# A two-layer Mamba and attention kernel: four pairs of vector calls merged, a convolution history copied by DMA, integer weights converted by ScalarE

## The chip, the cores and the metric

The kernel runs on one core of one Trainium2 chip. The metric is the device time of one execution in microseconds, lower is better. A core has five engines with an instruction queue each: TensorE (PE in the profile, with its weight loads as PEld), VectorE (DVE), ScalarE (ACT), GpSimd (POOL) and SyncE (SP). In this kernel SP issues all DMA transfers. Each engine works through its queue in order and waits for the others by semaphores.

## The reference, cut to what matters

The input `x` has 2 sequences of 2048 tokens with 256 features. Two layers are applied, each as `x = x + s * silu(g)`, where `s` is a sequence mixer and `g` a feed-forward network, both on the normalised `x`.

```python
# layer 0: s = a Mamba block and an MLP, g = an FFN in blockwise FP4 (blocks of 16)
xz = ln(xn) @ in_proj_w;  xi, z = split(xz, 2)              # 512 channels
xc = silu(causal_conv(xi, conv_w, 4 taps) + conv_b)
dt, B, C = split(xc @ x_proj_w, [16, 32])
dt = softplus(dt @ dt_proj_w + dt_proj_b)
h_t = exp(dt_t * A) * h_{t-1} + dt_t * B_t * xc_t           # 512 channels x 16 states, over 2048 steps
y = (sum_n h_t * C_t + D * xc) * silu(z)
s = x' + gelu(ln(x') @ ffn_w1 + b1) @ ffn_w2 + b2           # x' = xn + y @ out_proj_w
g = fp4_linear(silu(fp4_linear(xn, w_gate)) * fp4_linear(xn, w_up), w_down)
x = x + s * silu(g)
# layer 1: s = attention over the first axis (2 positions) with 16 heads, g = three QLoRA blocks
s = attention(xn)
for k in range(3):                                           # weight = (q / 7.5 - 1) * scale, plus a LoRA term
    h = h + qlora(gelu(ln(qlora(h, 2 * k))), 2 * k + 1)
x = x + s * silu(h)
```

The four taps of the convolution reach three tokens back, so each tile of tokens needs the last three columns of `xi` of the tile before: this is the convolution history. The integers `q` of the QLoRA weights come as int32.

## The kernel before

Time is cut into 8 tiles `j` of 256 tokens, for each of the 2 sequences `b`: 16 stages in the order (0,0), (0,1), (1,0) and so on. A stage has these parts:

- `head`: normalisation, input projection, convolution (as matmuls of `xi` with diagonal matrices `cdiag`), `xc`, `dt`, `ux`, and `bc`, the B and C rows, which go to a scratch in DRAM. It runs a stage ahead of the rest. The history of each sequence is kept in the constant tile `hist[b]`; `head` copies it into the first three columns of `xi`, and the last three columns of `xi` back into it.
- `fp4_half`: quantisation of `xn` and the FP4 network. It leaves `sgs`, the `silu(g)` of the two groups of 128 tokens.
- `scan`: 8 scans per stage, 128 in all. For each, SP loads `bcs` (B and C, spread over the partitions), ACT makes `decay` in eight calls, and DVE makes three large calls on `hh`: a product with `ux`, the scan, and a product with C. Then PE transposes the result into `bank_y`, and SP saves the last column into `state` for the next tile. There are two buffers each of `bcs`, `decay` and `hh`.
- `tail`: second normalisation and MLP. Its last lines form layer 0's result `x1` as `sg * s + xt`, with one product and one sum for each group of 128 tokens.
- `second`: layer 1 for 128 tokens of both sequences, twice after each stage with b = 1, so 16 times. The attention part multiplies the queries `pq` of the two sequences by a difference of keys, reduces, takes tanh, multiplies by a difference of values and adds a mean of values.

Ahead of the stages, weights are prepared: FP4 weights are quantised on the chip, and `make_qlora_weights` turns six int32 tiles into float, scales them and folds the LoRA product in.

No engine's order is written out by hand. The class `Recorder` records all calls with their stage; `order` then plans them with a list of costs for each kind of call (`cost`), and issues them in the order of the plan. It starts from priorities by stage (`lead`, `adjust`) and repeats a backward and a forward pass over the recorded calls for each entry of `passes`; the last forward pass gives the order. An entry holds the weights of that pass: among them how much a change of the table on ACT counts against a call (`bonus`), and shifts for single parts of a stage. A change of ACT's function table is planned at `SWITCH = 1.41` us. All recorded calls are issued from one line (579), so the profile tells them apart by the names of their tiles, not by line.

The tiles are allotted by the plan: `sg` has two buffers of 128x256, `xi` has one.

Of the kernel before, what the change touches and what calls it, by code (L numbers as in the profile page):

```python
# [8 lines left out]
F32 = mybir.dt.float32  # L9
I32 = mybir.dt.int32  # L10
BF16 = mybir.dt.bfloat16
AF = mybir.ActivationFunctionType
ALU = mybir.AluOpType
# [4 lines left out]
P = 128  # L18
D = 256
# [3 lines left out]
T = 256  # L23
TG = T // P
FI = 704
FH = FI // 2
BLK = 16
# [555 lines left out]
def tile_two_layers(ctx: ExitStack, tc: tile.TileContext, a: dict):  # L583
    nc = tc.nc
    rec = Recorder(nc, ctx.enter_context(tc.tile_pool(name="shadow", bufs=1, space=DRAM)))
    x = a["x"]
    out = a["out"]
    B, L, _ = x.shape
# [6 lines left out]
    tmp = rec.pool(ctx.enter_context(tc.tile_pool(name="tmp", bufs=1)), 1)  # L595
# [6 lines left out]
    def bank(stream, name):  # L602
        tag = USES.get(stream, stream)
        return ps.tile([P, 512], F32, tag=f"bank_{tag}", name=name, bufs=BANKS[tag], group=stream)
# [24 lines left out]
    def load(name, shape, src):  # L629
        t = const.tile(shape, F32, tag=name, name=name)  # L630
        rec.sync.dma_start(t, src)
        return t
# [77 lines left out]
    hist = [const.tile([P, 4, 3], F32, tag=f"hist{b}", name=f"hist{b}") for b in range(B)]  # L710
# [150 lines left out]
    def make_qlora_weights():  # L861

        scl = load("q_scl", [P, 6, 2, D // BLK], a["scales"].rearrange("i (c p) n -> p i c n", p=P))
        wl = const.tile([P, 6, 2, D], F32, tag="w_l", name="w_l")
        for i in range(6):
            qi = tmp.tile([P, 2, D], I32, tag="t2k_s0", name=f"qi_{i}", bufs=depth["s0"])
            rec.sync.dma_start(qi, a["qweights"][i].rearrange("(c p) d -> p c d", p=P))
            lab = t2k("s0", f"lab_{i}")
            rec.sync.dma_start(lab[0:32, 0:D], a["lora_a"][i])
            rec.sync.dma_start(lab[0:32, D : 2 * D], a["lora_bt"][i])  # L870
            w = t2k("s1", f"wq_{i}").rearrange("p (c d) -> p c d", c=2)
            rec.vector.tensor_copy(w, qi)
            rec.vector.tensor_scalar(w, w, 1.0 / 7.5, -1.0, ALU.mult, ALU.add)
            for c in range(2):
                wv = w[:, c, :].rearrange("p (n k) -> p n k", k=BLK)
                rec.vector.tensor_tensor(
                    wv, wv, scl[:, i, c, :].unsqueeze(2).to_broadcast([P, D // BLK, BLK]), ALU.mult
                )
            for dc in range(2):
                pw = bank("s0", f"pl_{i}_{dc}")  # L880
                rec.tensor.matmul(
                    pw[:, :D], lhsT=lab[0:32, dc * P : (dc + 1) * P], rhs=lab[0:32, D : 2 * D],
                    start=True, stop=False,
                )
                for oc in range(2):
                    rec.tensor.matmul(
                        pw[:, oc * P : (oc + 1) * P], lhsT=w[:, oc, dc * P : (dc + 1) * P],
                        rhs=ident, start=False, stop=(oc == 1),
                    )
                if i % 2:  # L890
                    rec.scalar.copy(wl[:, i, dc, :], pw[:, :D])
                    continue

                mv = statistics("s0", pw[:, :D].unsqueeze(1), 1, f"l_{i}_{dc}")
                rec.vector.tensor_scalar(
                    wl[:, i, dc, :], pw[:, :D], mv[:, 0, 0:1], None, ALU.subtract
                )
        wt["l"] = wl


    def head(b, j, xt):
        nm = f"{b}_{j}"
# [16 lines left out]
        xi = mam.tile([P, 4, T + 3], F32, tag="xi", name=f"xi_{nm}", bufs=1)  # L919
        if j == 0:  # L920
            rec.vector.memset(xi[:, :, 0:3], 0.0)
        else:
            rec.vector.tensor_copy(xi[:, :, 0:3], hist[b])
        for pr in range(2):
            px = bank("m", f"px_{nm}_{pr}").rearrange("p (m t) -> p m t", m=2)
            for mm in range(2):
# [5 lines left out]
                    )  # L932
            rec.scalar.copy(xi[:, 2 * pr : 2 * pr + 2, 3:], px)
        if j < NJ - 1:
            rec.vector.tensor_copy(hist[b], xi[:, :, T : T + 3])
        xc = mam.tile([P, 4, T], F32, tag="xc", name=f"xc_{nm}", bufs=1)
        for pr in range(2):
            pc = bank("m", f"pc_{nm}_{pr}").rearrange("p (m t) -> p m t", m=2)
# [10 lines left out]
        pd = bank("m", f"pxp_{nm}")  # L949
# [107 lines left out]
    def fp4_half(b, j, h):  # L1057

        nm = f"{b}_{j}"
        sgs = []  # L1060
        q = fp4(h["xn"].rearrange("p g d -> p (g d)"), TG * D, f"x{nm}")
        pt = transpose_pair("q", q.rearrange("p (g d) -> p g d", g=TG), f"q{nm}")
        xq = t2k("q", f"xq_{nm}").rearrange("p (c t) -> p c t", c=2)
        rec.scalar.copy(xq, pt)
        for g in range(TG):
            hb = tmp.tile([P, FI], F32, tag="h", name=f"h_{nm}_{g}", bufs=2)
            for hf in range(2):
                w0 = hf * FH
                both = []
                for key in ("w_gate", "w_up"):  # L1070
                    pg = bank("f", f"p{key}_{nm}_{g}_{hf}")
                    for c in range(2):
                        rec.tensor.matmul(
                            pg[:, :FH], lhsT=xq[:, c, g * P : (g + 1) * P],
                            rhs=wt[key][:, c, w0 : w0 + FH], start=(c == 0), stop=(c == 1),
                        )
                    both.append(pg)
                hg = hb[:, w0 : w0 + FH]
                rec.scalar.activation(hg, both[0][:, :FH], AF.Silu)
                rec.vector.tensor_tensor(hg, hg, both[1][:, :FH], ALU.mult)  # L1080
            q = fp4(hb, FI, f"h{nm}_{g}")
            hq = tmp.tile([P, NW, P], F32, tag="hq", name=f"hq_{nm}_{g}")
            for k0, k1 in ((0, 4), (4, NW)):
                pt = bank("f", f"ph_{nm}_{g}_{k0}").rearrange("p (k t) -> p k t", k=4)
                for k in range(k0, k1):
                    rec.tensor.transpose(pt[:, k - k0, :], q[:, CUT[k] : CUT[k] + P], ident)
                rec.scalar.copy(hq[:, k0:k1, :], pt[:, : k1 - k0, :])
            pd = bank("f", f"pdn_{nm}_{g}")
            for k in range(NW):
                rec.tensor.matmul(  # L1090
                    pd[:, :D], lhsT=hq[:, k, :], rhs=wt["w_down"][:, k, :],
                    start=(k == 0), stop=(k == NW - 1),
                )
            sg = tmp.tile([P, D], F32, tag="sg", name=f"sg_{nm}_{g}", bufs=2)
            rec.scalar.activation(sg, pd[:, :D], AF.Silu)
            sgs.append(sg)
        return sgs

    def tail(b, j, h, x2, sgs, x1):
        nm = f"{b}_{j}"  # L1100
# [11 lines left out]
        for fp in range(4):  # L1112
            ph = bank("f", f"ph_{nm}_{fp}").rearrange("p (f t) -> p f t", f=2)
            gl = t2k("f", f"gl_{nm}_{fp}").rearrange("p (f t) -> p f t", f=2)
            for ff in range(2):
                f = 2 * fp + ff
# [5 lines left out]
            for ff in range(2):  # L1122
                f = 2 * fp + ff
# [3 lines left out]
            for ff in range(2):  # L1127
                f = 2 * fp + ff
# [5 lines left out]
        s = t2k("f", f"s_{nm}").rearrange("p (g d) -> p g d", g=TG)  # L1134
        rec.vector.tensor_tensor(s, pf.rearrange("p (g d) -> p g d", g=TG), x2, ALU.add)

        for g in range(TG):
            sg = sgs[g]
            rec.vector.tensor_tensor(sg, sg, s[:, g, :], ALU.mult)
            rec.vector.tensor_tensor(x1[:, g, b, :], sg, h["xt"][:, g, :], ALU.add)  # L1140


    def second(j, g, x1):
        nm = f"{j}_{g}"
# [41 lines left out]
        dkv = t2k(st, f"dkv_{nm}")  # L1186
# [3 lines left out]
        pq = bank(st, f"pq_{nm}")  # L1190
# [3 lines left out]
        vm = bank(st, f"pvm_{nm}")[:, :D]  # L1194
        bias_row(vm, 32, 2 * D, D)
        for c in range(2):
            for bb in range(B):
                rec.tensor.matmul(
                    vm, lhsT=ht[:, c, bb * P : (bb + 1) * P], rhs=wt["qkv"][:, c, 2 * D :],
                    start=False, stop=(c == 1 and bb == B - 1),  # L1200
                )
        ct = t2k(st, f"ct_{nm}")
        e = small.tile([P, 2 * NS], F32, tag="at_e", name=f"e_{nm}", bufs=2)
        for s in range(2):
            rec.vector.tensor_tensor(
                ct[:, s * D : (s + 1) * D], pq[:, s * D : (s + 1) * D], dkv[:, 0:D], ALU.mult
            )
        rec.vector.tensor_reduce(e, ct.rearrange("p (h d) -> p h d", d=BLK), AX.X, ALU.add)
        rec.scalar.activation(e, e, AF.Tanh, scale=0.5 * float(BLK) ** -0.5)
        for s in range(2):  # L1210
            cs = ct[:, s * D : (s + 1) * D]
            rec.vector.tensor_tensor(
                cs.rearrange("p (h d) -> p h d", d=BLK),
                dkv[:, D : 2 * D].rearrange("p (h d) -> p h d", d=BLK),
                e[:, s * NS : (s + 1) * NS].unsqueeze(2).to_broadcast([P, NS, BLK]), ALU.mult,
            )
            rec.vector.tensor_tensor(cs, cs, vm, ALU.add)
        pt = transpose_pair(st, ct.rearrange("p (b d) -> p b d", b=B), f"d{nm}")
        ctt = t2k(st, f"ctt_{nm}").rearrange("p (c t) -> p c t", c=2)
        rec.scalar.copy(ctt, pt)  # L1220
# [83 lines left out]
    h = head(0, 0, x_first)  # L1304
    rec.stage = (0, QUANT)
    make_fp4_weights()
    for i, (j, b) in enumerate(order):
        if b == 0:
            x1 = mam.tile([P, TG, B, D], F32, tag="x1", name=f"x1_{j}")
# [6 lines left out]
        sgs = fp4_half(b, j, h)  # L1316
# [11 lines left out]
        h = following  # L1328
# [32 lines left out]
        (20, 0.5, 0.1, 0.5, 0.12, [(11, 3, 'tensor', 0.138), (3, 0, 'tensor', -0.771), (5, 0, 'scalar', 0.427)]),  # L1361
        (80, 0.1, 0.05, 2, 0.08, []),
        (20, 1, 0.1, 0.5, 0.12, []),
    ]
    rec.issue(tc, lead=(12.22, -6.26, 0, -7.42, 1.15), bonus=193.318, ahead=0.034, adjust=adjust, passes=passes)

# [47 lines left out]
```

## Time and profile before

| | us |
|---|---|
| median of 3 runs | 1744.28 (1741.94 to 1745.17) |
| the profiled execution: its own time | 1740.26 |
| its span (first to last instruction) | 1738.5 |
| DVE busy | 1629.0 (94%) |
| PE busy | 1554.3 (89%) |
| ACT busy | 1472.7 (85%), of it 467.0 table loads (364) |
| first scan, last scan (start) | 56.8, 1609.2 |

Busy is the time in which an engine had at least one instruction in work. In a row for a group of instructions, the name left of the arrow is the tile written and those to the right are read; after the first bar stand the busy time of the group in us and the mean of one instruction in ns, after the second the idle time of the engine just ahead of them and what ended it. A row of the windows gives, for a stretch, the busy time of each engine, with the number of instructions in brackets, then TensorE's granted clock, the share of the DMA engines and GB/s.

### The profile page before, as it was taken

The page shows a single profiled execution, that of the slowest core. Times are in us where ns is not written, and L with a number is a line of the kernel's source. Part 1 is how long each engine was busy: PE and PEld are TensorE (multiplying, and loading weights), DVE is VectorE, ACT ScalarE, POOL GpSimd, SP SyncE. Part 2 cuts the span into 40 slices and gives each one's busy share as a digit, 9 for nine tenths or more (in the row PEclk, how much of TensorE's full clock was granted, in tenths as well). Part 3 has the DMA queues.
Part 4 walks back from the last instruction along what each step waited for, and adds up shares of the span by engine and source line. Part 5 has one row for each costly group of instructions (what it writes and reads, how often), then busy time and mean ns, then how long its engine had stood idle before and what let it go on. Part 6 is the DMA issues. An engine that isn't in the chain of part 4 may idle for free.

```text
span 1738.5 us, 22023 instructions
## 1 busy us (share of the span) xinstructions
PE 1554.3 (89%) x7948; PEld 1224.5 (70%) x7948; DVE 1629.0 (94%) x1658; ACT 1472.7 (85%) x2903; POOL 180.2 (10%) x122
## 2 busy tenths in 40 slices
PE   7546978899899999989998999999899989997996
PEld 5335757687686868678785777787676767776765
DVE  8999999999999999999999999999999999999623
ACT  6546877779899999989998989999999998999443
POOL 0000100111110111100101002110202011200000
PEclk9768989999999999999999999999999999999999
DMA  7322121212212222222222221222122121111000
GB/s 182 94 57 49 39 55 44 49 40 55 42 50 62 37 52 48 56 43 50 50 50 62 48 45 46 54 43 56 38 49 50 44 56 43 50 43 50 6 6 13
DMA packets 179467, 87.23 MB, mean 50 GB/s; under 512 B 131575, under 2 KB 145565, under 8 KB 179358
## 3 DMA queue, kind: packets, MB, share of 16 engines
q1 hardware_dynamic: 179358, 85.83, 21.3%
q8 instruction: 62, 1.02, 0.2%
q14 instruction: 47, 0.39, 0.1%
HBM read 80.62 MB, written 4.72 MB: 49 GB/s over the span
## 4 chain that ended last, share of the span: by engine, by line
PE 28%; DVE 19%; ACT 11%; issue 6%; POOL 0%; ACTq 0%; DVEq 0%
DVE hh L579 13%; PE bank_f L579 11%; PE bank_m L579 6%; PE bank_s L579 5%; PE bank_y L579 4%; ACT L579 4%; ACT decay L579 3%; ACT t2k_s L579 2%; PE bank_h L579 2%; DVE fp_l L579 2%; DVE fp_sc L579 1%; DVE t2k_s L579 1%; ACT t2k_f L579 1%; DVE h L579 1%; ACT dt L579 0%
## 5 line engine op out<-in xcount | busy, mean ns | idle before, releaser
L579 DVE TENSOR_TENSOR_SCAN hh<-decay,hh 128x2056 f32<-128x2056 f32 x128 | 567.3, 4432 | 4.0 <-ACT decay L579 1.9
L579 ACT ACT_TABLE_LOAD x364 | 467.0, 1283 | 22.0 <-DVE hh L579 8.2
L579 ACT ACTIVATE decay<-dt,amat 128x256 f32<-128x256 f32 x1024 | 443.4, 501 | 48.8 <-DVE hh L579 47.2
L579 PE MATMUL bank_y<-ident,hh 128*128 128x128 f32 x2048 | 280.3, 283 | 48.1 <-DVE hh L579 43.4
L579 PEld LDWEIGHTS bank_y<-ident,hh 128*128 128x128 f32 x2048 | 246.1, 146 | 86.8 <-issue 43.8
L579 DVE TENSOR_TENSOR hh<-ux,bcs 128x2048 f32<-128x2048 f32 x128 | 291.7, 2279 | 2.9 <-PE bank_y L579 2.7
L579 DVE TENSOR_TENSOR hh<-hh,bcs 128x2048 f32<-128x2048 f32 x128 | 292.0, 2282 | 0.4
L579 POOL TENSOR_TENSOR ln_sq_s<-ln_sq_s,power 128x2 f32<-128x2 f32 x42 | 73.1, 1741 | 713.6 <-ACT ln_sq_s L579 713.6
L579 PE MATMUL bank_f<-w_f,t2k_f 128*128 128x256 f32 x512 | 129.6, 384 | 6.8 <-ACT t2k_f L579 6.7
L579 PE MATMUL bank_f<-t2k_f,w_f 128*128 128x256 f32 x512 | 122.9, 381 | 1.4 <-ACT t2k_f L579 1.1
L579 PE MATMUL bank_m<-xi,cdiag 128*128 128x256 f32 x512 | 123.5, 379 | 0.7 <-ACT xi L579 0.7
L579 PEld LDWEIGHTS bank_f<-w_f,t2k_f 128*128 128x128 f32 x512 | 93.2, 191 | 25.5 <-ACT t2k_f L579 11.7
L579 PEld LDWEIGHTS bank_f<-t2k_f,w_f 128*128 128x128 f32 x512 | 95.3, 190 | 18.1 <-ACT t2k_f L579 3.7
L579 PEld LDWEIGHTS bank_m<-xi,cdiag 128*128 128x128 f32 x512 | 94.4, 190 | 15.5 <-ACT xi L579 1.1
L579 PE MATMUL bank_f<-w_down,hq 128*128 128x256 f32 x384 | 97.7, 393 | 4.7 <-ACT hq L579 4.6
L579 PE MATMUL bank_h<-t2k_s,w_l 128*128 128x256 f32 x360 | 88.6, 385 | 9.9 <-ACT t2k_s L579 9.9
L579 DVE SCALAR_TENSOR_TENSOR fp_l<-fp_h,fp_l 128x704 f32<-128x704 f32 (+2 forms) x124 | 91.5, 738 | 5.2 <-ACT fp_h L579 4.6
L579 PE MATMUL bank_f<-w_gate,t2k_f 128*128 128x352 f32 x256 | 91.7, 479 | 4.9 <-ACT t2k_f L579 3.1
L579 PE MATMUL bank_f<-w_up,t2k_f 128*128 128x352 f32 x256 | 90.0, 468 | 6.7 <-DVE h L579 3.7
L579 PEld LDWEIGHTS bank_f<-w_down,hq 128*128 128x128 f32 x384 | 73.3, 197 | 22.5 <-ACT hq L579 8.7
L579 PE MATMUL bank_s<-w_qkv,t2k_s 128*128 128x256 f32 (+1 forms) x280 | 83.8, 432 | 4.0 <-DVE t2k_s L579 4.0
L579 PE MATMUL bank_s<-w_l,t2k_s 128*128 128x256 f32 x336 | 82.6, 384 | 4.5 <-ACT t2k_s L579 4.5
(191 smaller groups left out, 2454.5 us busy)
## 6 DMA issues: line engine op xcount, KB each, us to landing
bcs<-bc SPq DMA_DIRECT2D x128, 512.0 KB, 4.8
xt<-in_x_dram SPq DMA_DIRECT2D x16, 256.0 KB, 3.8
out_dram<-t2k_s SPq DMA_DIRECT2D x15, 256.0 KB, 2.2
w_f<-in_ffn_w_dram SPq DMA_DIRECT2D x2, 1024.0 KB, 9.7
state<-hh SPq DMA_DIRECT2D x112, 4.0 KB, 2.3
t2k_s<-in_qweights_dram SPq DMA_DIRECT2D x6, 256.0 KB, 5.9
w_in<-in_in_proj_w_dram SPq DMA_DIRECT2D x1, 1024.0 KB, 5.4
h<-in_w_gate_dram SPq DMA_DIRECT2D x6, 128.0 KB, 2.2
```

What stands on the lines that cost most here:

```text
L579: getattr(getattr(self.nc, engine), method)(*args, **kwargs)
```

## The change

1. `tail`: product and sum of layer 0's end are made for both groups in one call each. `sgs` is one tile of 128x2x256 with one buffer instead of two of 128x256.
2. `second`: the product of queries and keys and the sum with `vm` are made for both sequences in one call each; the operand that both share is spread by a stride of zero. The product with `e` stays in two calls.
3. `head`: the copies of the history into and out of `xi` become DMA transfers on SP (14 each way; the first tile of a sequence still has a memset).
4. `make_qlora_weights`: the conversion of the integers moves from DVE to ACT (6 calls).
5. `passes` gets five more entries, so the plan is another one for all engines.

```diff
@@ make_qlora_weights
-            rec.vector.tensor_copy(w, qi)
+            rec.scalar.copy(w, qi)
@@ head
-            rec.vector.tensor_copy(xi[:, :, 0:3], hist[b])
+            rec.sync.dma_start(xi[:, :, 0:3], hist[b])
...
-            rec.vector.tensor_copy(hist[b], xi[:, :, T : T + 3])
+            rec.sync.dma_start(hist[b], xi[:, :, T : T + 3])
@@ fp4_half
-        sgs = []
+        sgs = tmp.tile([P, TG, D], F32, tag="sg", name=f"sg_{nm}", bufs=1)
...
-            sg = tmp.tile([P, D], F32, tag="sg", name=f"sg_{nm}_{g}", bufs=2)
-            rec.scalar.activation(sg, pd[:, :D], AF.Silu)
-            sgs.append(sg)
+            rec.scalar.activation(sgs[:, g, :], pd[:, :D], AF.Silu)
@@ tail
-        for g in range(TG):
-            sg = sgs[g]
-            rec.vector.tensor_tensor(sg, sg, s[:, g, :], ALU.mult)
-            rec.vector.tensor_tensor(x1[:, g, b, :], sg, h["xt"][:, g, :], ALU.add)
+        rec.vector.tensor_tensor(sgs, sgs, s, ALU.mult)
+        rec.vector.tensor_tensor(x1[:, :, b, :], sgs, h["xt"], ALU.add)
@@ second
-        for s in range(2):
-            rec.vector.tensor_tensor(
-                ct[:, s * D : (s + 1) * D], pq[:, s * D : (s + 1) * D], dkv[:, 0:D], ALU.mult
-            )
+        rec.vector.tensor_tensor(
+            ct.rearrange("p (s d) -> p s d", s=2), pq.rearrange("p (s d) -> p s d", s=2),
+            dkv[:, 0:D].unsqueeze(1).to_broadcast([P, 2, D]), ALU.mult,
+        )
...
-            rec.vector.tensor_tensor(cs, cs, vm, ALU.add)
+        rec.vector.tensor_tensor(
+            ct.rearrange("p (s d) -> p s d", s=2), ct.rearrange("p (s d) -> p s d", s=2),
+            vm.unsqueeze(1).to_broadcast([P, 2, D]), ALU.add,
+        )
@@ passes
         (20, 1, 0.1, 0.5, 0.12, []),
+        (30, 0.02, 0.02, 1, 0.05, []),
+        (80, 1, 0.05, 1, 0.12, []),
+        (110, 0.1, 0.0, 1, 0.12, []),
+        (30, 1, 0.0, 1, 0.05, [(11, 3, 0.08)]),
+        (30, 0.3, 0.0, 0.3, 0.08, [(0, 3, 'scalar', 0.793), (0, 4, 'gpsimd', 0.705), (12, 4, 'tensor', -0.188), (14, 4, 'tensor', 1.073), (9, 4, 'vector', -0.14)]),
```

More of the change, by code (lines that the diff above doesn't have):

```diff
@@ L1210, in second @@
         for s in range(2):
-            cs = ct[:, s * D : (s + 1) * D]
             rec.vector.tensor_tensor(
-                cs.rearrange("p (h d) -> p h d", d=BLK),
+                ct[:, s * D : (s + 1) * D].rearrange("p (h d) -> p h d", d=BLK),
                 dkv[:, D : 2 * D].rearrange("p (h d) -> p h d", d=BLK),
```

## The prediction

> **What bounds the kernel now.** I read four views in this order: the page's busy shares, the table of windows (busy time by stretch), the waits of the Vector engine, and the chain of waits at the end.
>
> ```profile
> PE 1554.3 (89%) x7948; PEld 1224.5 (70%) x7948; DVE 1629.0 (94%) x1658; ACT 1472.7 (85%) x2903; POOL 180.2 (10%) x122
> ```
>
> DVE leads, but three engines are close, and an average hides the stages. The windows (busy us, then the number of instructions in brackets) cut the span into start, three parts of the main stretch, and end:
>
> ```profile
> 0.00:57.00 57.00, 45.89 (x216) 33.88 (x216) 47.64 (x163) 38.09 (x77) 4.12 (x15) 1.00 0.70 181
> 57.00:450.00 393.00, 306.66 (x1496) 237.38 (x1497) 389.44 (x338) 288.44 (x565) 30.44 (x25) 0.88 0.21 49
> 450.00:1200.00 750.00, 712.65 (x3739) 569.18 (x3737) 738.54 (x683) 703.50 (x1383) 82.15 (x44) 0.99 0.23 49
> 1200.00:1605.00 405.00, 374.56 (x1984) 296.54 (x1983) 393.92 (x353) 385.74 (x770) 54.60 (x26) 1.00 0.20 49
> 1605.00:1739.00 134.00, 114.56 (x516) 87.52 (x516) 59.51 (x125) 56.90 (x112) 8.90 (x12) 0.93 0.03 8
> ```
>
> Columns three to six are PE, PEld, DVE and ACT. From 57 us (first scan) to 1605 us DVE works 1521.9 of 1548 us, 98%: there a microsecond taken from DVE is a microsecond of time, unless another engine takes its place. The next is ACT: 73% busy up to 450 us, but 94% and 95% after it. The waits of DVE inside 57 to 1605 us are short and mostly on PE; none names a DMA:
>
> ```profile
> DVE t2k_s L579 <- PE bank_s L579: 4.6, 4, 2.4
> DVE hh L579 <- PE bank_y L579: 2.7, 3, 1.6
> DVE hh L579 <- ACT decay L579: 1.9, 2, 1.2
> ```
>
> The last 134 us are another regime: DVE 44% busy, PE 85%. In the chain PE runs without a break for most of 1605 to 1670 us, and then two instances of `second` run out as a chain of short steps over all engines:
>
> ```profile
> 1655.30 1.74 PE bank_f L579 x8
> 1657.06 0.48 ACT t2k_f L579
> 1657.59 12.35 PE bank_f L579 x56
> ```
>
> [...] The trace has the 1283, but between an ACT instruction and the load after it the chain shows 0.02 us, so I price a load at 1.28. [...]
>
> **The change part by part.** Counts are those of the two built programs' instruction lists; prices are these rows (busy and mean ns stand after the bar):
>
> ```profile
> L579 DVE TENSOR_TENSOR sg<-sg,t2k_f 128x256 f32<-128x256 f32 x32 | 12.8, 418 | 0.1
> L579 DVE TENSOR_TENSOR x<-sg,xt 128x256 f32<-128x256 f32 x32 | 12.8, 416 | 0.1
> L579 DVE TENSOR_TENSOR sz<-bank_y,sz 128x512 f32<-128x512 f32 x32 | 21.8, 683 | 0.4 <-PE bank_y L579 0.2
> L579 DVE CAST t2k_s<-t2k_s 128x512 f32<-128x512 int32 x6 | 2.5, 418 | 0.0
> L579 DVE COPY xi<-hist 128x12 f32<-128x12 f32 x14 | 2.3, 164 | 0.0
> L579 DVE COPY hist<-xi 128x12 f32<-128x12 f32 x14 | 2.2, 155 | 0.4 <-ACT xi L579 0.4
> L579 ACT ACT_TABLE_LOAD x364 | 467.0, 1283 | 22.0 <-DVE hh L579 8.2 <-PE bank_f L579 3.8 <-PE bank_h L579 1.7
> L579 ACT ACTIVATE fp_h<-fp_l 128x512 f32<-128x512 f32 x16 | 10.0, 627 | 0.1
> ```
>
> 1. DVE, 98 instructions fewer. Durations overlap: in the timeline the next instruction starts about 0.08 us before the end of the one before, so from start to start a 256-wide one takes 0.34, a 512-wide one 0.60, a 12-wide copy 0.10 and a conversion 0.38 us. Four merges of 32 into 16 calls: 64 x (0.68 - 0.60) = 5. Conversions: 6 x 0.38 = 2.3. History: 28 x 0.10 = 2.8. Together 10; by the rows' means it would be up to 17, the upper bound. A broadcast operand already stands in the two large `hh` products at the plain rate, so I add nothing for it.
> 2. ACT, 6 copies of 128x512 more at up to 0.63: under 4 us. Nobody wrote the other addition: the planner issues everything in a new order, and in it ACT loads its table 398 times instead of 364. 34 x 1.28 = 44; together +47.
> 3. SP, 28 DMAs more, 14 reading and 14 writing `hist`. SP is in order. It mostly waits for `hh` products, and an issue takes it about 0.4 us, so the issues themselves (11 us) cost nothing. The landing, by the nearest row, is 2.3 us instead of the copy's 0.16. The write has a whole stage of time. The read has to be in `xi` before the convolution matmuls, next to the two ACT copies into the same tile, but it waits until the head before has finished with `xi`.
>
> ```profile
> bcs<-bc SPq DMA_DIRECT2D x128, 512.0 KB, 4.8
> state<-hh SPq DMA_DIRECT2D x112, 4.0 KB, 2.3
> ```
>
>    Behind a waiting read stand the next `state` and `bcs` transfers, and for `bcs` waits the product that opens a scan. In the timeline the shortest time from the end of a product with `bcs` to the start of the one that needs the refilled buffer is 5.7 us, often 6.6 to 7; issue and landing take 5.2. The cover is thin where scans follow each other closely. In the new order, nearly all reads stand one scan or more after the matmuls they wait for, so I take 0, with bounds of 0 and 14 x 1.5 = 21. A gain is excluded, as no transfer is taken away.
> 4. POOL keeps its 127 instructions, PE its 5610.
> 5. Where the new order puts the work, summed from start-to-start durations. Ahead of the first scan DVE has 39 us instead of 45. The first scan also needs `bcs`, which landed at 53 us just ahead of the 54.2 us start; of its 12 earlier queue entries since `bc` 7 remain, so it should come sooner, but I count 2 us of the 6 as lost. After the last scan starts, DVE has the same (51). PE, from the transposes of the third scan from the end, has 119 us instead of 111: the second `second` of j=6 begins later. About 4 us of it fit into gaps in which PE waited after 1600 us. So +4.
> 6. Stalls of DVE. In stretches of 8 scans ACT's own work was at most 103.3 us where DVE had 93.9; now the worst is 103.8 against 97.9. Counting how far ACT's and PE's work runs ahead of DVE's, scan by scan, beyond a slack of 8 us, the sum falls from 37 to 27 (ACT) and from 57 to 41 (PE): ACT has more work, laid more evenly. The planner also charges 1.41 us for a table load that takes 1.28, so ACT should be early rather than late by its plan. I take -2 of today's 26 us of stalls; bounds -10 and +20.
>
> Sum: -10 (DVE) +2 (start) +4 (end) -2 (stalls) = -6 us. The profiled execution took 1740.26 us (span 1738.5 and 1.8 around it), which gives 1734. The median of the three runs, 1744.28, is 4.0 above it; the same difference on that gives **1738**. Where cover is gone: with 35 of the 47 us after 450 us, ACT has some 25 us of idle time left of 65, and the next late thing would be `decay`.
>
> **The rivals.**
> A. ScalarE becomes the bound (slower). After 450 us ACT idles 65 of 1155 us, most of that waiting for PE results that no reordering removes. If only half of the added 35 us finds room, the other 17 stretch the main part: -6 + 17 = +11, 1755 us. For it: in 1200 to 1605 us, where ACT is at 95%, DVE falls from 98.5% to 97.3%. Against it: the scan-by-scan count above, and DVE's waits on `decay` are only 1.9 us. It decides from 6 us of lost room.
> B. The new history reads hold SP's queue and `bcs` comes late. Against it: DVE never waits for `bcs` today. If a third of the 14 reads cost 1.5 us each: +7, 1745 us.
> C. The end eats it: the extra 8 us on PE count in full, and the later start of `second` adds another 2 of chain: -10 + 2 + 10 - 2 = 0, 1744 us. For it: PE is saturated there.
> D. The plan keeps DVE fuller than I think (10 us of stalls gone): -14, 1730 us.
>
> **How the numbers follow.** Forecast 0.40, D 0.17, A 0.22, B 0.09, C 0.12. About 0.2%, 3.5 us, is what a measurement of this kernel can tell from no change. Faster by more: the forecast and D, but for the forecast's edge near 1741: 0.55. Same: that edge, C and part of B: 0.17. Slower: A and the rest of B: 0.28. The range takes in D with the larger DVE saving and A: 1726 to 1756; the likeliest side alone is 1726 to 1741.
>
> **What would show it.** DVE busy about 1617 us with 1560 instructions; ACT busy about 1519 with 398 loads; the last scan 8 to 12 us earlier; the time from it to the end some 4 us longer. I am wrong if DVE's waits on ACT (`decay`, `fp_h`, `at_e`) grow past 15 us (A), if DVE waits for DMA `bcs` (B), or if the last scan is 8 us earlier and the end is not (C).

## The result, and the profile after

The kernel after takes **1755.86 us** (median of 4 runs, 1755.06 to 1756.99) where the kernel before took 1744.72 in the same set: ratio 1.0066, 95% interval 1.0048 to 1.0083. It is slower by 0.66%, about 11 us. Its profiled execution took 1755.89 us, span 1754.0, so span stands against span as 1738.5 to 1754.0, +15.5. This is 4 us more than the difference of the medians, because the profiled execution of before lay 4 us under its median.

The busy shares first, the same line of the page as shown for before:

```profile
PE 1560.1 (89%) x7944; PEld 1234.8 (70%) x7948; DVE 1613.0 (92%) x1560; ACT 1520.7 (87%) x2943; POOL 175.7 (10%) x122
```

DVE has 16 us less to do and ACT 48 us more, where the prediction had 10 and 47. Then the windows (PE, PEld, DVE, ACT in columns three to six):

```profile
57.00:450.00 393.00, 312.97 (x1538) 242.93 (x1537) 390.31 (x338) 310.48 (x583) 22.25 (x24) 0.88 0.23 51
450.00:1200.00 750.00, 707.54 (x3712) 569.34 (x3714) 728.93 (x639) 724.02 (x1408) 84.96 (x46) 0.98 0.23 49
1200.00:1605.00 405.00, 373.48 (x1952) 296.20 (x1951) 386.26 (x329) 380.54 (x745) 55.32 (x25) 0.98 0.20 47
1605.00:1754.00 149.00, 126.98 (x585) 96.79 (x585) 66.44 (x119) 71.77 (x142) 9.02 (x13) 0.95 0.03 11
```

From 450 to 1605 us DVE fell from 98.1% busy to 96.6%. Work went away, and idle time took its place. The waits of DVE from 57 to 1605 us say for whom it idles:

```profile
DVE hh L579 <- PE bank_y L579: 16.0, 13, 4.7
DVE h L579 <- PE bank_f L579: 6.6, 5, 3.2
```

Each row gives the sum in us, the number of waits and the longest. The first was 2.7 us in 3 waits before, the second 2.2 us in 3; waits on `decay` are gone, and no wait on `bcs` has come. The rows of the merged calls and of the table loads:

```profile
L579 DVE TENSOR_TENSOR sg<-sg,t2k_f 128x512 f32<-128x512 f32 x16 | 10.9, 684 | 0.1
L579 ACT ACT_TABLE_LOAD x398 | 510.6, 1283 | 17.6 <-PE bank_h L579 3.4 <-PE bank_f L579 2.6 <-DVE hh L579 2.4
```

The merged calls cost what the row of a 512-wide call said: 684 ns against 683, and 676 and 675 where one operand is spread by a stride of zero. In the chain of waits there is something that the chain of before does not have: GpSimd's `ln_sq_s`.

```profile
1569.29 2.23 ACT decay L579 x6
1573.06 6.48 POOL ln_sq_s L579
...
1598.58 4.02 POOL ln_sq_s L579
```

`ln_sq_s` is the root of layer 1's normalisation, a call on 128x2 numbers.

The ledger of the traces, in us. It adds up: the last scan starts when VectorE's work and idle time before it are over. VectorE's work counts overlapping instructions once.

| | DVE work before the last scan | DVE idle before the first scan | DVE idle from the first to the last scan | last scan starts | from there to the end |
|---|---|---|---|---|---|
| before | 1573.7 | 9.4 | 26.2 | 1609.2 | 129.2 |
| after | 1557.8 | 16.0 | 45.9 | 1619.7 | 134.3 |

So 16 us of work went, 26 us of idle time came, 6.6 of it before the first scan, and the end is 5 us longer.

### The profile page after: what moved, and what is told of

It is laid out like the page before. It is cut to its first block, busy times and chain, and to the rows that moved or that the text cites. A ratio compares the mean times of both kernels' runs of the same rounds, so it can differ in the third digit from the quotient of the medians.

```text
span 1754.0 us, 22010 instructions
## 1 busy us (share of the span) xinstructions
PE 1560.1 (89%) x7944; PEld 1234.8 (70%) x7948; DVE 1613.0 (92%) x1560; ACT 1520.7 (87%) x2943; POOL 175.7 (10%) x122
## 4 chain that ended last, share of the span: by engine, by line
PE 45%; DVE 29%; ACT 16%; issue 8%; POOL 1%; DMA 1%; ACTq 0%; DVEq 0%
DVE hh L579 19%; PE bank_f L579 17%; PE bank_m L579 11%; PE bank_s L579 8%; PE bank_y L579 6%; ACT L579 6%; ACT decay L579 4%; DVE fp_l L579 3%; PE bank_h L579 2%; ACT t2k_s L579 2%; DVE fp_sc L579 1%; DVE t2k_s L579 1%; ACT t2k_f L579 1%; POOL ln_sq_s L579 1%; DVE h L579 1%
## 5 line engine op out<-in xcount | busy, mean ns | idle before, releaser
L579 PE MATMUL bank_y<-ident,hh 128*128 128x128 f32 x2048 | 287.0, 284 | 46.6 <-DVE hh L579 46.5
L579 POOL TENSOR_TENSOR ln_sq_s<-ln_sq_s,power 128x2 f32<-128x2 f32 x42 | 83.3, 1984 | 738.1 <-ACT ln_sq_s L579 738.1
L579 PE MATMUL bank_h<-t2k_s,w_l 128*128 128x256 f32 x360 | 97.7, 415 | 19.8 <-ACT t2k_s L579 19.6
L579 PEld LDWEIGHTS bank_h<-t2k_s,w_l 128*128 128x128 f32 x360 | 69.2, 205 | 40.6 <-ACT t2k_s L579 29.1
L579 PE MATMUL bank_f<-w_down,hq 128*128 128x256 f32 x384 | 92.9, 383 | 1.4 <-ACT hq L579 1.2
```

What stands on the lines that cost most here:

```text
L579: getattr(getattr(self.nc, engine), method)(*args, **kwargs)
```

## The experiments

The change mixes edits and a new order, so the two were separated by replaying. `order` was made to write down its result (the sequence of calls, and the buffer of each tile); other kernels then follow that list instead of planning:

```diff
-        order, _ = self.order(**how)
+        order = self.follow(plan, slots)    # recorded from the kernel before, or after
```

A merged call stands where the first of its two stood, a call whose operands aren't there yet goes as soon as they are. The added lines move the one issuing line to L671, L695, L726 or so. Single executions vary (the kernel before ran from 1737 to 1754 us over all sets), so each ratio is to the runs of before on the same chip.

| label | calls | order | us | ratio, 95% interval |
|---|---|---|---|---|
| f_all | all edits | before | 1747.14 | 1.0030 (1.0019 to 1.0041) |
| f_merge | merges only | before | 1741.46 | 0.9995 (0.9987 to 1.0003) |
| f_hist | history by DMA only | before | 1747.16 | 1.0027 (1.0017 to 1.0036) |
| f_histw | history writes by DMA only | before | 1747.19 | 1.0021 (1.0010 to 1.0032) |
| f_hist1 | f_hist, writes of j=0 on DVE | before | 1744.35 | 1.0012 (0.9998 to 1.0025) |
| f_conv | conversion on ACT only | before | 1748.09 | 1.0016 (1.0003 to 1.0030) |
| f_loads | none, 36 more table loads | before | 1792.04 | 1.0286 (1.0268 to 1.0304) |
| b_less | none, 34 fewer table loads | before | 1742.51 | 0.9996 (0.9987 to 1.0005) |
| b_pe | none, two taps fewer | before | 1746.13 | 0.9992 (0.9978 to 1.0005) |
| g_none | no edit | after | 1751.85 | 1.0051 (1.0039 to 1.0063) |
| g_less | none, 34 fewer table loads | after | 1753.22 | 1.0058 (1.0042 to 1.0074) |
| g_pe | none, two taps fewer | after | 1761.21 | 1.0093 (1.0066 to 1.0120) |
| g_recip | none, six roots on DVE | after | 1753.79 | 1.0065 (1.0048 to 1.0082) |
| a_recip | all edits, six roots on DVE | after | 1747.21 | 1.0022 (1.0012 to 1.0032) |
| a_nohist | all but the history | after | 1757.43 | 1.0077 (1.0052 to 1.0103) |
| x_oldpass | all edits | planned by the 18 old passes | 1768.33 | 1.0152 (1.0130 to 1.0174) |

### Edits or order

> All four edits, but every engine's queue in the order of the kernel before (no planning: the old order is replayed, merged calls stand where the first of the two stood). Theory 1 (the new order is the loss, through ScalarE's 34 extra table loads and later deliveries to TensorE): faster than before by the DVE work taken away, 10 to 16 us, about 1732; table loads 364. Theory 2 (the edits themselves cost, history reads on SP or the conversion on ACT at the start): slower than before, up to +11, about 1750 to 1756. If it is within 3 us of before, the DVE work taken away turned into waits even in the old order.

> None of the four edits, but every engine's queue in the order of the kernel after (replayed; split calls stand next to each other). Theory 1 (order): slower than after by the DVE work that comes back, 1756 + 5 to 16 = 1761 to 1772, with 398 table loads. Theory 2 (edits): back at before's 1745. If DVE's extra stalls in the new order are slack made by other engines, its work fills them and the time stays near 1756.

Both cost. The new order with the old calls is 0.51% slower (9 us), and the edits in the old order are 0.30% slower (5 us). Theory 1 was right that the order loses and wrong that the edits gain. In f_all VectorE has 5.2 us less to do before the last scan, but idles 12 us more (47.8 instead of 35.6), 6.5 of it before the first scan.

### The merges

> The merged calls of tail and second alone, in the order of before. By start-to-start durations 64 x (0.68 - 0.60) = 5 us less, by row means 9: 1735 to 1740 where DVE paces; no change if merging only moves the wait for the second half (the merged product starts when both halves are there).

Neither end of it: 0.05% faster, not told apart from no change. In the trace, the time from each of these calls to the start of the next one was summed over the four main groups: 42.6 us before (120 calls) and 39.9 with them merged (60 calls); waits in front of the next call are in both sums. So 2.6 us, half of the 5 in the prediction. In three of the groups a merged call held DVE for 0.62 to 0.66 us on average until the next one started, not for 0.60; in the trace of after, the next call starts 0.72 or 0.73 us after a merged product when it reads all of its result (seven times), and mostly 0.58 to 0.61 us after it when it does not. Before, the other half of the product could stand between. It is also the fastest version tried that computes everything; none beats the kernel before by more than the measurement can tell.

### The history

```diff
-            rec.vector.tensor_copy(hist[b], xi[:, :, T : T + 3])
+            rec.sync.dma_start(hist[b], xi[:, :, T : T + 3])     # f_hist, f_histw; f_hist1: only for j > 0
```

> The history by DMA alone, in the order of before. Free (prediction's step 3): -3 to -4.5 us, about 1741. Rival B (reads hold SP's queue, bcs late): +7 or more, about 1752, with waits of DVE for DMA bcs in the trace.

> Order of before; the history is written by DMA (14 on SP), read by VectorE as before. If the write is what costs (it waits in SP's in-order queue behind weight loads and holds the only xi buffer until it has landed, so ScalarE's next copy into xi waits): nearly all of f_hist's loss, first scan 3 to 5 us later than before's 56.8, time about 1746 to 1747. If the reads cost (rival B as predicted): first scan unchanged, time about 1742 to 1743.

> Order of before; history by DMA both ways, but the two writes of j=0, which fall in the start when SP issues weight loads without a break, stay on VectorE. If the loss is the start's queue: first scan within 1 us of 56.8 and time 1741 to 1744 (what is left is f_hist's other 1.6 us of later waits less VectorE's 26 copies). If every write costs alike: 12/14 of the loss stays, about 1746.

The write costs; for the reads no price shows: f_histw has nearly all of f_hist's loss (the difference is inside the intervals), and no wait of DVE names `bcs`. The timeline of f_hist has the place, first SP's queue, then ACT's (start, duration, and in brackets the wait in front):

```profile
37.42 0.73 SPq L671 DMA_DIRECT2D l_bet<-in_ln_beta_dram  x1
38.25 0.77 SPq L671 DMA_DIRECT2D hist<-xi  x1
```

```profile
40.55 0.59 ACT L671 COPY xi<-bank_m 128x512 f32<-128x512 f32 x1 [3.56 <-DMA hist<-xi]
```

`xi` of the first tile was complete at 19.7 us, but the write stands in SP's queue behind the weight loads that SP issues one after the other in the start. In before, SP's transfers follow each other there from 29.5 to 50.9 us without a gap of more than 0.12 us, and one load alone held the queue for 5.47 us. `xi` has one buffer, so the next `head` may fill it only when the write has landed: ACT waits 3.56 us, the convolution and the table loads behind it move, and the first scan starts at 61.5 instead of 56.8 us. With the two writes of j=0 back on DVE (f_hist1) the first scan is at 56.7 and nothing waits for a DMA of `hist`; the rest, +0.12%, isn't told apart from nothing. By time alone f_hist1 isn't told apart from f_hist either (the intervals meet); it is the traces that place the loss in the start.

> The kernel after in its own order, with the history back on VectorE (28 small copies, no DMA). If the history's DMAs cost in the new order as in the old one: 3 to 5 us faster than after, about 1751. If they are free there (first scan of after and g_none are within 0.1 us): VectorE's 28 copies come back, +0 to +3, unless they shift the two GpSimd roots at the end out of VectorE's scan, which would give up to -8.

In the new order the history's DMAs show no price: taking them out of the kernel after gains nothing (1.0077 against 1.0066, the intervals overlap and could hide some 0.2%), and nothing in the trace of after waits for `hist`. The same edit costs 0.27% in one order and nothing that shows in another.

### The conversion

> The integer conversion on ScalarE alone, in the order of before. By the sum of the other edits (f_all 4.2 less f_hist 4.2 plus f_merge -1.4): +1 to +2, about 1745; prediction's step 1 and 2: -2 from VectorE, nothing from ScalarE, 1741 to 1742. A later first scan with a wait of VectorE for ACT t2k_s would show the cost.

About +2.8 us, with an interval that nearly reaches nothing. In the trace VectorE waits 2.5 us for ACT `t2k_s` in the start, and the first scan starts at 60.9 us instead of 56.8; TensorE's granted clock up to 57 us was 0.97 there instead of 1.00, so whether that wait is the whole price isn't shown. In the new order no price shows: VectorE waits 3.12 us for `t2k_s` in the start of after, but the first scan starts at 57.2, and at 57.3 in g_none, which converts on DVE.

### ScalarE's table loads

```diff
+                if i in extra:      # f_loads: 20 places, 36 loads
+                    self.nc.scalar.activation(dum, eps, extra[i])
+                if i in less:       # b_less, g_less: 17 short runs of another table
+                    args[2] = AF.Identity
```

> Calls and order of before, with 20 tiny activations (128x1, into a tile nobody reads) of another function put into ScalarE's queue, spread as the extra work of the new order is: 36 more table loads, 400 in all, 46 us of loads and about 4 us of activations. If ScalarE's load is what makes the new order slow: about as slow as the new order with the old calls, +7 to +12, 1750 to 1755. If ScalarE has room for it (prediction's step 6): within 3 us of before, 1743 to 1746; then the order's loss has another cause.

> Old calls in the order of before, 17 short runs made Identity in the same way: 330 loads instead of 364, 44 us less. Says whether ScalarE's loads are on the path of before too: f_loads lost 48 us for 50 added. VectorE idles only 26 us between first and last scan, so the gain is bounded by about 26: if ScalarE paces together with VectorE, 1720 to 1735; if it has been hidden behind VectorE all along, 1741 to 1745.

> Old calls in the order of after (as g_none, 1751.85), but 17 short runs of silu, gelu or tanh-gelu between calls of another table become Identity (values change, the calls and their sizes stay): 364 table loads, as before, instead of 398, 44 us less. If the 34 loads are the price of the new order (rival A): at or below before's time, 1735 to 1745. If the order loses elsewhere (end +4, start, TensorE): no more than 3 us of it comes back, 1748 to 1752.

Adding 50 us to ACT in the old order costs 48, far outside both numbers expected, so at these places ACT had no room for work that the plan doesn't know of. But taking 44 us away gains nothing in either order. The busy shares of g_none and then g_less show that the work really went:

```profile
PE 1558.0 (89%) x7948; PEld 1230.4 (70%) x7948; DVE 1622.3 (93%) x1658; ACT 1517.3 (87%) x2937; POOL 173.7 (10%) x122
```

```profile
PE 1560.9 (89%) x7948; PEld 1234.5 (71%) x7948; DVE 1622.3 (93%) x1658; ACT 1473.8 (84%) x2903; POOL 174.5 (10%) x122
```

This speaks against rival A, the slower side of the prediction: with as many loads as before, the new order is as slow as with 34 more. It isn't the last word. The 17 places are spread over the kernel and are not those at which the new order added its loads, and between scan 119 and the last none was taken (19 loads in g_none and in g_less, 22 in before). That the plan had put its loads where ACT could bear them fits the three runs, but is argued.

### TensorE

In the trace of g_none, DVE idles 16.0 us more than in before up to the last scan (51.6 instead of 35.6), and its waits on PE between the first and the last scan grow from about 12 to 23 us. A typical one, PE's queue in the timeline:

```profile
593.40 1.25 PE L671 MATMUL bank_y<-ident,hh 128*128 128x128 f32 x10
594.49 0.63 PE L671 MATMUL bank_f<-w_f,t2k_f 128*128 128x256 f32 x2
...
600.79 1.03 PE L671 MATMUL bank_f<-w_f,t2k_f 128*128 128x256 f32 x4
601.65 0.60 PE L671 MATMUL bank_f<-ident,fp_l 128*128 128x128 f32 x4
602.09 1.15 PE L671 MATMUL bank_y<-ident,hh 128*128 128x128 f32 x9
```

and DVE's:

```profile
602.95 2.29 DVE L671 TENSOR_TENSOR hh<-ux,bcs 128x2048 f32<-128x2048 f32 x1 [2.67 <-PE bank_y L671]
```

PE doesn't wait here; 7.6 us of other work, mostly matmuls of the MLP and of layer 1, stand between the first transposes into `bank_y` and the next ones, and DVE needs that buffer for the next scan. Is it PE's amount of work?

```diff
-                for k in range(4):
+                for k in (0, 3):        # b_pe, g_pe: two of the four taps
```

> Order and calls of before, two of the convolution's four taps left out (128 matmuls of 0.44 us, 56 us of TensorE, spread over the 16 heads; values change). If TensorE is not what VectorE waits for in this order: within 3 us of before, 1740 to 1744.

> Old calls in the order of after (g_none, about 1752 to 1753), the same taps left out. If the new order's loss is TensorE's work standing ahead of what VectorE waits for (its waits on PE grow from 9 to 21 us between first and last scan): falls by 6 us or more further than b_pe does, to 1740 to 1746. If the loss is the end and the start alone: as little as b_pe, 1749 to 1753.

This was **inconclusive**. PE's busy time fell by only 34 and 27 us instead of 56 (256 of the 512 records of `bank_m<-xi,cdiag` are left out, and in before 32 of them take 7.08 us), while the granted clock from 450 to 1200 us went from 0.99 to 0.98 in b_pe and 0.97 in g_pe, and g_pe came out slower than g_none. A lighter PE gained nothing that can be told, but a slower clock was part of the experiment. In b_pe it shows in the start too: up to 57 us the granted clock was 0.82 instead of 1.00, and the first scan started at 63.5 us instead of 56.8.

The clock itself is a rival that no run separates. The five executions of g_none were granted 0.956 of the clock on average, the 46 of before in the same set 0.959; but among the 43 of before in another set the fastest (1738.22 us) had 0.966 and the slowest (1753.83 us) 0.956, with one and the same order. Whether a lower clock makes an execution longer or comes with it is not shown.

### GpSimd

```diff
-                rec.gpsimd.tensor_tensor(y, y, power[:, :B], ALU.pow)
+                rec.vector.reciprocal(y, y)     # for j = 6 only, six calls
```

> The kernel after in its own order, but the six inverse roots ln_sq_s of layer 1 for j=6 are made by VectorE as plain reciprocals (1/v in place of v to the -0.5, so layer 1's values for j=6 change) instead of by GpSimd. In the trace of after two of them took GpSimd 6.47 and 4.01 us because VectorE was in a scan, and ScalarE waited 4.5 and 2.5 us for them. If that is what loses VectorE's lead at the end: ScalarE's waits for POOL ln_sq_s after 1570 us go, the last scan starts 6 to 8 us earlier, time 1748 to 1750. If the chain has other work as late: no more than 2 us, 1754 to 1756.

> Control for a_recip: old calls in the order of after (g_none, 1751.85), the six roots of j=6 as reciprocals on VectorE. In the trace of g_none these six take GpSimd 1.0 to 1.7 us and nobody waits for them. If a_recip's gain of 8 us is the two long ones of after: no change here, 1750 to 1754. If GpSimd roots cost in general: 1744 to 1747.

In these two kernels the six calls of j=6 give the reciprocal instead of its root. This is the clearest result. On the edited calls it gains 0.44% (1.0066 to 1.0022, 7.7 us), on the old calls in the same order nothing that can be told (1.0051 and 1.0065, the intervals overlap). The roots of g_none, and then those of after, in the timeline:

```profile
1579.41 1.62 POOL L671 TENSOR_TENSOR ln_sq_s<-ln_sq_s,power 128x2 f32<-128x2 f32 x1 [8.47 <-ACT ln_sq_s L671]
1598.61 1.29 POOL L671 TENSOR_TENSOR ln_sq_s<-ln_sq_s,power 128x2 f32<-128x2 f32 x1 [17.57 <-ACT ln_sq_s L671]
```

```profile
1573.06 6.47 POOL L579 TENSOR_TENSOR ln_sq_s<-ln_sq_s,power 128x2 f32<-128x2 f32 x1 [10.82 <-ACT ln_sq_s L579]
1598.58 4.01 POOL L579 TENSOR_TENSOR ln_sq_s<-ln_sq_s,power 128x2 f32<-128x2 f32 x1 [19.05 <-ACT ln_sq_s L579]
```

And what followed in after, on ACT, PE and DVE:

```profile
1579.57 0.84 ACT L579 ACTIVATE t2k_s<-bank_s,ln_sq_s 128x256 f32<-128x256 f32 x2 [4.50 <-POOL ln_sq_s L579]
```

```profile
1580.46 0.66 PE L579 MATMUL bank_s<-ident,t2k_s 128*128 128x128 f32 x4 [2.73 <-ACT t2k_s L579]
...
1591.31 1.91 PE L579 MATMUL bank_y<-ident,hh 128*128 128x128 f32 x16
```

```profile
1593.26 2.29 DVE L579 TENSOR_TENSOR hh<-ux,bcs 128x2048 f32<-128x2048 f32 x1 [4.68 <-PE bank_y L579]
```

The root runs long, ACT and everything behind it in its queue waits, PE gets `t2k_s` and `t2k_f` late, the transposes of `hh` come late, and DVE stands still for 4.68 us. One more step lies between: TensorE idled 2.73 and 1.51 us here, and from 1582 to 1588 us its granted clock was 0.50, where g_none and a_recip have 1.00. The same six matmuls in after and then in g_none:

```profile
1582.73 2.93 PE L579 MATMUL bank_f<-w_f,t2k_f 128*128 128x256 f32 x6 [1.51 <-ACT t2k_f L579]
1584.50 1.53 PE L671 MATMUL bank_f<-w_f,t2k_f 128*128 128x256 f32 x6
```

Counted from 0, scan 123 of after starts 6.4 us ahead of that of g_none (1574.6 against 1581.0); this was the gain of the edits. Scan 127, the last, starts 1.9 us behind (1619.7 against 1617.8). a_nohist shows the same two roots at 6.46 and 3.87 us, g_less and g_pe the short ones, so it isn't a chance of one execution.

g_recip leaves the roots of earlier tiles alone, and one of them is in the way in both kernels. In g_none:

```profile
1432.49 5.89 POOL L671 TENSOR_TENSOR ln_sq_s<-ln_sq_s,power 128x2 f32<-128x2 f32 x1 [15.12 <-ACT ln_sq_s L671]
```

ACT waits 3.61 us for it, then DVE 2.34 us for PE `bank_f`, and from scan 112 to scan 120 DVE idles 7.9 us where before has 3.1. Over the whole span ACT's waits for `ln_sq_s` are 1.1 us in before, 5.0 in g_none, 12.0 in after and 3.6 in a_recip. So a part of the 9 us of the order may be of this kind; no run took that root out.

### The added passes

> All four edits, planned by the 18 old passes alone, so a third order (405 table loads by its list). If the five added passes are what makes after slow: 1738 to 1748. If it is the edits, or more than 364 loads in any order: 1752 or more.

The edits planned by the 18 old passes alone give 1768.33 us. So the five passes help, against planning the edited calls without them. The edited calls run fastest in the order of before (f_all, 1.0030).

## Why the prediction was wrong, by its own steps

It forecast 6 us less, and the kernel takes 11 us more. The sixth term, VectorE's stalls, failed most; the start in the fifth failed too.

1. **DVE, -10.** 15.9 us went before the last scan, for two reasons. With the order alone DVE's work fell by 7.5 (1573.7 to 1566.2). That is mostly more overlap of neighbours: over the whole span its busy time fell by 6.7, the sum of all its durations by 2.3 only (1739.6 to 1737.3). The edits took 8.4 in the new order (1566.2 to 1557.8) and 5.2 in the old one. The size of the edits was about right, the term of the merges was half of what it was put at, and the overlap that came with the order was not in the term.
2. **ACT, +47.** 48.0 measured, 398 loads. DVE's waits on ACT did not grow past 15 us for the three tiles that it named, and taking as many loads out again (g_less) gave nothing back.
3. **History, 0.** No price of the reads shows, as worked out. "The write has a whole stage of time" was wrong: its buffer has no stage of time, since `xi` is single, and in f_hist ACT waits 3.56 us for it. That SP mostly waits, so that the issues cost nothing, isn't so in the start, where its transfers follow each other up to 50.9 us in before. In this new order no price of the miss shows; in the old one it is +0.2%.
4. **POOL and PE, counts unchanged.** True, and yet a miss. A count says nothing of GpSimd's duration: two calls of the same count and shape took 7.6 us longer (6.47 and 4.01 instead of 1.62 and 1.29).
5. **Start +2, end +4.** The end is 5.1 us longer; that was right, and g_none alone has 4.1 of it (133.3 instead of 129.2). The start was not. The +2 meant that the first scan would come 4 us earlier, as DVE had 6 us less to do ahead of it. DVE did have 6.2 us less (41.2 instead of 47.4), but idled 6.6 us more, and the first scan came 0.4 us later: the term measures +6.6. `bcs` was not sent sooner either: it was issued at 48.30 us instead of 48.08, because `bc` ahead of it went out at 43.00 instead of 39.81. The chain of waits to the first scan of after runs for 8.44 us through PE `bank_m`, and in the first part of it TensorE was at about half its clock. The windows of before, then of after:

```profile
38.00:48.00 10.00, 10.00 (x54) 8.45 (x53) 5.49 (x19) 8.08 (x21) 0.00 (x0) 1.00 0.33 77
38.00:48.00 10.00, 4.76 (x12) 3.55 (x13) 4.72 (x17) 8.08 (x21) 0.00 (x0) 0.55 0.12 16
```

   g_none has 0.51 there, so it comes with the order. What it costs no run shows.
6. **Stalls, -2, with bounds -10 and +20.** This is the step that failed most. Between the first and the last scan DVE idled 45.9 us instead of 26.2: +19.7, at the upper bound. 11.1 of it come with the order (g_none, 37.3), and 8.6 more with the edits in it. From scan 120 to the last, DVE idled 0.9 us in before, 1.2 in g_none and 9.3 in after, and 1.3 in a_recip: this part is shown to come from GpSimd's roots of j=6. I had counted how far ACT's and PE's work ran ahead of DVE's in stretches of 8 scans. That can't see what stands in front of one transpose inside a stretch, and it left GpSimd out.

Put side by side, the four terms DVE, start, end and stalls were -10, +2, +4, -2 and measure -15.9, +6.6, +5.1, +19.7, which makes the +15.5 of the spans.

Of the rivals, A had the right side and nearly the right time (1755), but by luck: its cause, too many loads on ACT, is not what g_less shows. The range reached up to 1756 for A's sake, so that the result lies just inside it is luck too. B put the history's price on the reads and `bcs`; it sits on the write and `xi`, and only in the old order. C put the end at +10, twice what it measured. D went the other way. The slow way that decided was not among them: edits that gain about 6 us on DVE, given back because a small call on a helper engine ended only behind a scan and took 6.47 us instead of 1.62.

What stays open is which placements make the new order 9 us slower with the old calls. Shown by a run: as many loads as in before don't mend it. From the traces only: between before and g_none the end grew by 4 us, the idle time before the first scan by 4.9 and that between the scans by 11.1, against 7.5 us less work of DVE. Most of the idle time between the scans is waits for PE; one long root of GpSimd stands in front of some of them. The experiment on PE didn't settle it.

## What to carry to other kernels

When an edit also makes a planner issue everything anew, replay the old order with the new calls and the new order with the old calls before you explain anything: here each was slower, the edits for the history and the conversion in the start, the order for reasons that are only partly known. Room on an engine is not the time that it idles: 50 us put in at 20 fixed places cost 48, and 44 taken out at 17 others gained nothing. An engine with little to do can still set the time: GpSimd was busy for 10% of the span, and with six of its calls moved to VectorE, two of them of 6.47 and 4.01 us, the kernel took 7.7 us less. Look at how long its calls took, not only at how many there are. The DMA put in place of a copy held its source buffer until it had landed, and ACT waited 3.56 us for `xi`: look at who refills that buffer and at what is ahead in the queue, above all in the start.

## What the runs showed of the hardware

GpSimd's roots took 0.70 us on 128x2 numbers and 1.01 us on 128x4 when VectorE was idle throughout (medians of 139 and 9 calls in the 18 traces). Of 319 that began while VectorE was in a scan, the median ended 0.49 us after that scan; of 477 that began in a large product on `hh`, most ended 0.56 us after the product, but 17, at four places of the program, ended over 4 us after it, behind the scan that followed as well. Why a root ends behind a call of VectorE, and why these 17 didn't end behind the first one, is not shown: in g_none the root started 1.06 us before the end of a product and ended 0.56 us after it, in after it started 1.03 us before the end and ended 5.44 us after it, and the same two calls of VectorE followed in both, each starting before the last one had ended.

With 56 us of matmuls left out the granted TensorE clock was lower (0.99 to 0.97 in the middle of g_pe), and only 34 and 27 of the 56 us left PE's busy time. Twice in after a stretch at half the clock (0.50 from 40 to 48 us and from 1582 to 1588 us) began while TensorE idled. The first time it had waits of 5.50 and 1.44 us, and then 16 matmuls into `bank_m` took 6.28 us (in before 12 of them took 2.76); the second time the waits were 2.73 and 1.51 us, and six matmuls took 2.93 us instead of 1.53.
